# Layer 0: a term of TensorE's sum split between VectorE's partial sum and GpSimd's adds

## The chip, the cores and the metric

The kernel runs on one core of a Trainium2 chip. The metric is the device time of one execution in microseconds (us). The core has five engines that run their own instruction queues in order: TensorE (PE in the profile, with its weight loads as PEld), VectorE (DVE), ScalarE (ACT), GpSimd (POOL) and SyncE (SP), which here only issues transfers. They meet at semaphores.

## The reference, cut to what matters

Four layers are applied to x of shape (2, 64, 256, 256), each adding its result to x. The change is in layer 0. With _gn a group norm, _unfold3x3 nine copies of its input shifted by -2, 0 or 2 rows and columns (zero outside the image), and em an embedding of 64 channels made from an image and from positions:

```python
un_em = _unfold3x3(em)
feature_score = jnp.einsum('bckhw,bchw->bkhw', un_em, em)
un_fea = _unfold3x3(inp)
comp_score = jax.nn.sigmoid(jnp.einsum('bckhw,c->bkhw', un_fea, w_comp))
phi = comp_score * feature_score
weighted_fea = jnp.einsum('bckhw,bkhw->bchw', un_fea, phi)
...
x = x + _L0_conv_ref(_gn(x), L0_conv_img, L0_conv_w_pos, L0_conv_w_img, L0_conv_w_comp)
```

So for each of nine shifts the channels of em at a pixel are multiplied with those at the shifted pixel and summed to one score; the output is the sum over the shifts of score x g, where g is the input times its own sigmoid gate, taken at the shifted pixel.

## The kernel before, in words

The 128 partitions hold 2 images x 64 channels. Layer 0 goes over the image in 128 steps of two rows (nstep), so a tile of one step is 128 x 512 values, all float32. A score of a pixel and its neighbour is the same seen from either side, so of the nine shifts only five are computed: no shift, and A (0, 2), B (2, -2), C (2, 0), D (2, 2) in rows and columns (the dictionary shift). Each score of A to D is used twice. "term" is the score times g at the shifted pixel, for the pixel itself (mult, L366). "moved" is the score times the pixel's own g (move, L371), kept in padded tiles mvA to mvD, to be read later with the opposite shift (moved_to, L377) for the neighbour. A's neighbour is in the same two rows; those of B, C and D are in the next step's rows, so moved_to takes their tile of the step before.

One pass of the loop at L388 (index t) issues work of several stages:

- embed(t): TensorE's pl (L319) and pe (L321), ScalarE's sg and e (L325, L328), and at the end of the pass's GpSimd work the gate g = fea x sg (gated, L334). Every fourth step ScalarE first copies two halo rows of g and e (L317).
- products(t-2): ScalarE's square sq (L353), and on GpSimd the products of e with its four shifted views, pr (L356).
- step n = t-3: TensorE turns sq and the four pr into scores pf (score, L361: a matmul that sums over the channels of an image; it uses four PSUM buffers). VectorE multiplies: part = own g x score (L422), then for A, B, C, D the term and the moved tile. For A, VectorE also adds the term into part, in PSUM (L430), and then mvA and part into A's term tile (L431). So the shift of zero and both halves of A end in the one tile term A.
- step last = t-4: GpSimd adds the moved tile of the step before to the terms C, D and B, each in place (add, L381, in the order of L400). TensorE adds the four tiles A, C, D, B up in PSUM by matmuls with the identity (out, L405, tile acc). They are issued between the scores of step n. VectorE adds acc to x (yt, L438) and takes statistics (L439); yt goes out by a transfer (L440).

The order on every engine is the order in which these calls are written (L386 asks for a manual schedule). On GpSimd a pass is: C, D, B adds, four products, gate. On VectorE: part, A term, A moved, L430, L431, B term, B moved, C term, C moved, D term, D moved, yt, statistics: 13 operations. On TensorE: pl, pe, sq score, A score, acc A, B score, acc C, C score, acc D, D score, acc B: 11 matmuls. In float32 each shows as two matmul records and two weight loads.

part is one PSUM buffer, acc one, pf four. The term tiles come from a pool of 10, pr from 8, mvB, mvC and mvD from 3 each.

Of the kernel before, what the change touches and what calls it, by code (L numbers as in the profile page):

```python
# [18 lines left out]
C = 64  # L19
# [101 lines left out]
class Kernel:  # L121
# [115 lines left out]
    def layer0(self, x, y, coeffs):  # L237
# [3 lines left out]
        nc, tc, a = self.nc, self.tc, self.a  # L241
# [8 lines left out]
        with ExitStack() as ctx:  # L250
# [46 lines left out]
            xt, fea, sq, pr, term = {}, {}, {}, {}, {}  # L297
            inner = slice(2, 2 + W)

            def load(k):  # L300
                if 0 <= k < nblk:
                    xt[k] = pool.tile([P, R, W], F32, name="xt", bufs=3)
                    nc.sync.dma_start(xt[k], xv[:, R * k : R * k + R])
                    nc.sync.dma_start(rts[k % 2][32:38], rv[:, R * k : R * k + R])

            def features(n):
                k, s = divmod(n, per)
                fea[n] = pool.tile([P, 2, W], F32, name="fea")
                self.affine(fea[n], xt[k][:, 2 * s : 2 * s + 2], coeffs)

            def embed(n):
                k, s = divmod(n, per)
                g, e = gs[k % 2], es[k % 2]
                rows = slice(4 + 2 * s, 6 + 2 * s)
                if s == 0 and k:
                    for t in (gs, es):
                        nc.scalar.copy(t[k % 2][:, 2:4], t[1 - k % 2][:, R + 2 : R + 4])  # L317
                pl = p_l.tile([P, 2, W], F32, name="pl")
                nc.tensor.matmul(pl, wcomp, fea[n], start=True, stop=True)  # L319
                pe = p_e.tile([P, 2, W], F32, name="pe")  # L320
                nc.tensor.matmul(  # L321
                    pe, w_e, rts[k % 2][:, 2 * s : 2 * s + 2], start=True, stop=True
                )
                sg = pool.tile([P, 2, W], F32, name="sg")
                nc.scalar.activation(sg, pl, AF.Sigmoid)  # L325
                for i in range(2):
                    r = 2 * n + i
                    nc.scalar.activation(  # L328
                        e[:, 4 + 2 * s + i, inner],
                        pe[:, i],  # L330
                        AF.Identity,
                        bias=by_row[:, r : r + 1],
                    )
                return lambda: nc.gpsimd.tensor_tensor(  # L334
                    g[:, rows, inner], fea.pop(n), sg, ALU.mult
                )

            def at(n):

                k, s = divmod(n, per)  # L340
                if s == per - 1 and k + 1 < nblk:
                    return gs[(k + 1) % 2], es[(k + 1) % 2], 2
                return gs[k % 2], es[k % 2], 4 + 2 * s

            def near(t, j, name):
                dy, dx = shift[name]
                return t[:, j + dy : j + dy + 2, 2 + dx : 2 + dx + W]

            def products(n):
                _, e, j = at(n)  # L350
                own = e[:, j : j + 2, inner]
                sq[n] = pool.tile([P, 2, W], F32, name="sq")
                nc.scalar.activation(sq[n], own, AF.Square)  # L353
                for name in "ABCD":
                    t = pool.tile([P, 2, W], F32, name="pr", bufs=8)
                    nc.gpsimd.tensor_tensor(t, own, near(e, j, name), ALU.mult)  # L356
                    pr[n, name] = t

            def score(t):
                pf = p_f.tile([P, 2, W], F32, name="pf")  # L360
                nc.tensor.matmul(pf, self.block, t, start=True, stop=True)  # L361
                return pf

            def mult(n, name, in_, pf):
                t = pool.tile([P, 2, W], F32, name="term", bufs=10)
                nc.vector.tensor_tensor(t, in_, pf, ALU.mult)  # L366
                term[n, name] = t

            def move(n, name, own, pf):
                t = moved[name][n % len(moved[name])]  # L370
                nc.vector.tensor_tensor(t[:, :, inner], own, pf, ALU.mult)  # L371

            def moved_to(n, name):

                dy, dx = shift[name]
                n -= dy // 2
                return moved[name][n % len(moved[name])][:, :, 2 - dx : 2 - dx + W]  # L377

            def add(eng, n, name, other):
                t = term[n, name]  # L380
                eng.tensor_add(t, t, other)  # L381
# [4 lines left out]
            with tc.manual_schedule(engines={E.PE, E.DVE, E.Activation, E.Pool, E.SP}):  # L386
                features(0)
                for t in range(nstep + 5):  # L388
                    if t and t % per == 0:
                        load(t // per + 1)  # L390
                    gated = embed(t) if t < nstep else None
                    if t + 1 < nstep:
                        features(t + 1)

                    n, last = t - 3, t - 4
                    acc = None
                    if 0 <= last < nstep:
                        acc = p_o.tile([P, 2, W], F32, name="acc")
                        if last:
                            for name in "CDB":  # L400
                                add(nc.gpsimd, last, name, moved_to(last, name))

                    def out(name):
                        if acc is not None:
                            nc.tensor.matmul(  # L405
                                acc,
                                self.ident,
                                term.pop((last, name)),
                                start=name == "A",
                                stop=name == "B",  # L410
                            )

                    if 0 <= t - 2 < nstep:
                        products(t - 2)
                    if gated:
                        gated()
                    if 0 <= n < nstep:
                        g, _, j = at(n)
                        own = g[:, j : j + 2, inner]
                        pf = score(sq.pop(n))  # L420
                        part = p_s.tile([P, 2, W], F32, name="part")
                        nc.vector.tensor_tensor(part, own, pf, ALU.mult)  # L422
                        for i, name in enumerate("ABCD"):
                            pf = score(pr.pop((n, name)))
                            out("ACDB"[i])
                            mult(n, name, near(g, j, name), pf)
                            if name == "A" or n + 1 < nstep:
                                move(n, name, own, pf)
                            if name == "A":
                                nc.vector.tensor_add(part, term[n, name], part)  # L430
                                nc.vector.tensor_add(term[n, name], moved_to(n, name), part)  # L431
                    else:
                        for name in "ACDB":
                            out(name)
                    if acc is not None:
                        k, s = divmod(last, per)
                        yt = pool.tile([P, 2, W], F32, name="yt")
                        nc.vector.tensor_add(yt, xt[k][:, 2 * s : 2 * s + 2], acc)  # L438
                        nc.vector.bn_stats(stats[:, last, :], yt.rearrange("p r w -> p (r w)"))  # L439
                        nc.sync.dma_start(yv[:, 2 * last : 2 * last + 2], yt)  # L440
# [874 lines left out]
```

## Time and profile before

Three runs took 19660.62, 19662.92 and 19663.58 us: median 19662.92. The profiled execution took 19667.66 us, of which the span from its first to its last instruction is 19665.9.

| what | from the profile before |
|---|---|
| busy over the span | TensorE 74%, VectorE 94%, ScalarE 60%, GpSimd 82% |
| layer 0's steps | about 200 to 1458 us |
| adds of moved tiles (L381), GpSimd, 230 to 1440 us | mvC 1.09 us, mvD 1.27, mvB 1.27 each |
| products (L356), GpSimd | 1.13 us each on average |
| gate (L334), GpSimd | 1.27 us |
| VectorE's operations of a step | 0.68 to 0.70 us each |
| acc matmuls (L405), whole layer | 1024 records |
| granted TensorE clock, 300 to 1400 us | 1.00 |
| granted TensorE clock, whole span | 0.751 |

The page gives durations of single instructions as the profiler recorded them. Consecutive instructions of one engine overlap a little, so the pace of an engine is read from the distance between starts in the timeline, not from durations. In a line of the timeline the columns are start and length in us, engine, source line, operation, output <- inputs, form and count; a bracket at the end is the idle time before it and what ended it. Most of the span, some 14,000 us after layer 0, is layer 1, whose scan keeps VectorE busy; the shares over the whole span say little about layer 0.

### The profile page before, as it was taken

To read this page: it belongs to the slowest core of one execution; us is meant where nothing else is said; L and a number is where in the kernel's file an instruction comes from. 1 tells how busy PE (TensorE), PEld (TensorE's weight loads), DVE (VectorE), ACT (ScalarE), POOL (GpSimd) and SP (SyncE) were. 2 spreads that over 40 slices of the span, in tenths; PEclk is the share of its full clock that TensorE was granted. 3 is DMA by queue.
4 is the path that set the end of the run, shared out by engine and by line. 5 is a ranking of instruction groups with operands and counts; after the bars stand their busy time and mean duration, and the time that the engine had idled before them with its cause. 6 is when DMAs were issued, how large, how long until landed. Compare 5 with 4: busy or idle time off the path is not lost. (4 is left out here: it accounts for less than half of the span.)

```text
span 19665.9 us, 162715 instructions
## 1 busy us (share of the span) xinstructions
PE 14640.5 (74%) x48720; PEld 4861.7 (25%) x48720; DVE 18472.7 (94%) x16222; ACT 11804.0 (60%) x16810; POOL 16050.1 (82%) x8070
## 2 busy tenths in 40 slices
PE   7996767776777677767777677676777688888886
PEld 3431111111111111111111111111111154444444
DVE  6888999999999999999999999999999989999997
ACT  2226666666666666666666666666666555555554
POOL 6987888888888888888888888888888855555554
PEclk9996666666666666666666666666666698989898
DMA  3116666666666666666666666666666500000004
GB/s 124 54 50 157 151 151 151 153 149 156 149 154 152 151 151 151 155 147 157 151 153 150 151 152 151 156 148 154 154 150 151 126 28 29 30 30 29 29 27 145
DMA packets 662182, 2438.84 MB, mean 124 GB/s; under 512 B 131888, under 2 KB 201264, under 8 KB 450160
## 3 DMA queue, kind: packets, MB, share of 16 engines
q1 hardware_dynamic: 661296, 2428.43, 51.4%
q8 instruction: 385, 6.31, 0.1%
q14 instruction: 501, 4.10, 0.1%
HBM read 1990.14 MB, written 437.78 MB: 123 GB/s over the span
## 5 line engine op out<-in xcount | busy, mean ns | idle before, releaser
L792 DVE TENSOR_TENSOR_SCAN h<-da,st,h 128x512 f32<-128x512 f32 x8192 | 9838.6, 1263 | 308.2 <-ACT da L789 223.3
L796 POOL TENSOR_TENSOR h<-h,cb 128x2048 f32<-128x2048 f32 x2048 | 9253.1, 4518 | 164.9 <-POOL st L795 0.4
L789 ACT ACTIVATE da<-dl,p_a 128x512 f32<-128x512 f32 x8192 | 5565.3, 688 | 3985.5 <-DVE h L792 3891.2
L561 PE MATMUL py<-h,t_c_quad 128*32 128x512 f32 x16384 | 3253.7, 817 | 1649.1 <-POOL h L796 1648.6
L561 PE MATMUL pb<-bc,t_c_sel 64*128 64x512 f32 x3072 | 2697.0, 972 | 2385.5 <-DVE h L773 2379.9
L773 DVE TENSOR_TENSOR h<-dv,pb 128x2048 f32<-128x2048 f32 x1536 | 3472.3, 2261 | 40.9 <-DMA dv<-d_dv 40.9
L1021 POOL TENSOR_TENSOR gl<-gl,prod 128x512 f32<-128x512 f32 x1544 | 1959.0, 1270 | 1498.7 <-ACT prod L1017 1423.3
L755 POOL TENSOR_TENSOR h<-dv,cb 128x2048 f32<-128x2048 f32 x512 | 2318.7, 4529 | 17.1 <-DMA dl<-d_dl 17.1
L980 DVE SCALAR_TENSOR_TENSOR acc<-z,tap_b,acc 128x1024 f32<-128x1024 f32 (+1 forms) x1560 | 1988.4, 1275 | 38.8
L561 PEld LDWEIGHTS pb<-bc,t_c_sel 64*128 64x128 f32 x3072 | 661.6, 267 | 4411.3 <-DVE h L773 4345.9
L795 POOL COPY st<-h 128x4 f32<-128x4 f32 x2048 | 384.1, 188 | 1365.1 <-DVE h L792 1352.7
L561 PEld LDWEIGHTS py<-h,t_c_quad 128*32 128x32 f32 x16384 | 424.0, 122 | 3815.3 <-POOL h L796 3217.3
L561 PE MATMUL mm<-xin,p_conv 64*128 64x512 f32 x4096 | 1322.9, 775 | 15.2 <-DMA x1t<-y 15.2
L1064 PE MATMUL pcv<-z,diag 128*128 128x512 f32 x2322 | 1174.7, 623 | 19.8 <-ACT gl L1072 16.4
L949 ACT COPY z<-pz 128x512 f32<-128x512 f32 x768 | 456.4, 598 | 1034.1 <-PE pz L941 928.7
L1017 ACT ACTIVATE prod<-z,tap_a 128x512 f32<-128x512 f32 x1544 | 1045.1, 714 | 37.0 <-POOL gl L1021 36.8
L941 PE MATMUL pz<-t_c_inv,gf 128*128 128x128 f32 (+1 forms) x8192 | 1039.4, 309 | 1.9 <-DVE gf L922 1.9
L941 PEld LDWEIGHTS pz<-t_c_inv,gf 128*128 128x128 f32 (+1 forms) x8192 | 849.4, 181 | 520.0 <-issue 311.7
L561 PE MATMUL mm<-u,p_dt 128*128 128x512 f32 x1024 | 931.2, 1064 | 0.0
L561 PE MATMUL py<-u,p_d 128*128 128x512 f32 x1024 | 820.8, 894 | 0.0
L915 PE MATMUL f<-t_w_inT,xf 64*128 64x384 f32 x2048 | 596.7, 616 | 155.9 <-DVE gf L922 154.8
L561 PEld LDWEIGHTS mm<-xin,p_conv 64*128 64x128 f32 x4096 | 460.5, 244 | 982.6 <-issue 982.5
(167 smaller groups left out, 17448.8 us busy)
## 6 DMA issues: line engine op xcount, KB each, us to landing
cb<-d_bc SPq DMA_DIRECT2D x2048, 320.0 KB
dl<-d_dl SPq DMA_DIRECT2D x2048, 256.0 KB
dv<-d_dv SPq DMA_DIRECT2D x2048, 256.0 KB
d_dl<-delta SPq DMA_DIRECT2D x256, 512.0 KB
d_dv<-du SPq DMA_DIRECT2D x256, 512.0 KB
xin<-in_x SPq DMA_DIRECT2D x16, 2048.0 KB
xt<-in_x SPq DMA_DIRECT2D x32, 1024.0 KB
y<-yt SPq DMA_DIRECT2D x128, 256.0 KB
```

Source lines behind the costliest of these rows:

```text
L561: nc.tensor.matmul(out, lhsT, rhs, start=start, stop=stop)
L755: nc.gpsimd.tensor_tensor(h, t["dv", b], t["cb", b][:, 0].unsqueeze(1).to_broadcast([P, 4, T]), ALU.mult,)
L773: nc.vector.tensor_tensor(h, t["dv", b], pb.unsqueeze(1).to_broadcast([P, 4, T]), ALU.mult)
L789: nc.scalar.activation(da, t["dl", b][:, k], AF.Exp, scale=ws[m]["a"][:, k, j : j + 1])
L792: nc.vector.tensor_tensor_scan(h[:, k], da, h[:, k], state[m, b][:, j, k : k + 1], ALU.mult, ALU.add)
L796: nc.gpsimd.tensor_tensor(h, h, t["cb", b][:, 1 + j].unsqueeze(1).to_broadcast([P, 4, T]), ALU.mult)
L915: nc.tensor.matmul(p, x_f[t][half, g], w_in[half], start=True, stop=True)
L941: nc.tensor.matmul(pz[i * n : (i + 1) * n, k, :, 16 * g : 16 * g + 16], gf[t, 2 * e + g, b][:, c0 : c0 + n], inv, start=True, stop=True,)
L980: eng.scalar_tensor_tensor(out, near(s, name, m0, r, k), w, box["t"], ALU.mult, ALU.add)
L1017: nc.scalar.activation(prod, near(s, name, 4 * h + m, n, k), AF.Copy, scale=w)
L1021: nc.gpsimd.tensor_add(acc, acc, prod)
L1064: nc.tensor.matmul(box["t"], diag[:, k], near(s, f"a{i}", 4 * h + m, n, k), start=k == 0, stop=k == 8,)
```

## The change

B's term no longer has a tile of its own in TensorE's sum. In step n VectorE adds B's term to part in PSUM, as it does with A's. The add that makes the final A tile from mvA and part comes after that, behind B's term and B's moved tile. The moved tile of B, which GpSimd added to B's term, is now added to D's term, after mvD; GpSimd's adds stay three. TensorE sums A, C and D: A is issued behind the score of B instead of that of A, C behind that of C, D behind that of D, and D closes the sum.

```diff
-                            for name in "CDB":
-                                add(nc.gpsimd, last, name, moved_to(last, name))
+                            for name, moved_by in ("C", "C"), ("D", "D"), ("D", "B"):
+                                add(nc.gpsimd, last, name, moved_to(last, moved_by))
...
-                                stop=name == "B",
+                                stop=name == "D",
...
                         for i, name in enumerate("ABCD"):
                             pf = score(pr.pop((n, name)))
-                            out("ACDB"[i])
+                            if i:
+                                out("ACD"[i - 1])
                             mult(n, name, near(g, j, name), pf)
                             if name == "A" or n + 1 < nstep:
                                 move(n, name, own, pf)
-                            if name == "A":
+                            if name in "AB":
                                 nc.vector.tensor_add(part, term[n, name], part)
-                                nc.vector.tensor_add(term[n, name], moved_to(n, name), part)
+                            if name == "B":
+                                nc.vector.tensor_add(term[n, "A"], moved_to(n, "A"), part)
+                                term.pop((n, "B"))
                     else:
-                        for name in "ACDB":
+                        for name in "ACD":
                             out(name)
```

The tiles, pools and transfers are the same.

## The prediction

> **What bounds the kernel now.** The page says DVE 94% busy over the span, but that average belongs to layer 1. The change touches layer 0 alone, so I asked first for busy time by stretch, one stretch inside layer 0 and one inside layer 1. Columns: stretch, length, busy time of PE, PEld, DVE, ACT and POOL (with instruction counts), granted TensorE clock, DMA share, GB/s.
>
> ```profile
> 600.00:800.00 200.00, 200.00 (x449) 81.44 (x447) 168.02 (x266) 60.00 (x112) 185.57 (x163) 1.00 0.15 54
> 2000.00:3000.00 1000.00, 696.61 (x2052) 166.91 (x2052) 963.57 (x749) 655.27 (x893) 891.34 (x371) 0.69 0.66 152
> ```
>
> In layer 0 TensorE is busy 200 of 200 us at clock 1.00, GpSimd 93%, VectorE 84%. A busy TensorE isn't by itself a bound, so next the waits between 230 and 1440 us (total, times, longest):
>
> ```profile
> DVE part L422 <- PE pf L361: 148.1, 122, 1.2
> POOL term L381 <- DVE term L366: 84.2, 245, 0.4
> DVE term L366 <- PE pf L361: 19.9, 122, 0.2
> ```
>
> Once a step VectorE waits 1.2 us for TensorE's first score, and GpSimd waits twice for VectorE (0.28 and 0.41 us). TensorE's own waits (0.76 us ahead of the weights of pe and of sq) lie inside the 0.95 and 1.06 below. So the chain is TensorE, then VectorE, then GpSimd. TensorE's own timeline prices one step:
>
> ```profile
> 710.48 1.02 PE L319 MATMUL pl<-fea,wcomp 128*128 128x512 f32 x2
> 711.43 1.12 PE L321 MATMUL pe<-rt,w_e 38*128 38x512 f32 x2
> 712.49 1.13 PE L361 MATMUL pf<-sq,t_c_block 128*128 128x512 f32 x2
> 713.45 1.02 PE L361 MATMUL pf<-pr,t_c_block 128*128 128x512 f32 x2
> 714.31 1.02 PE L405 MATMUL acc<-term,t_c_ident 128*128 128x512 f32 x2
> ...
> 720.32 1.02 PE L319 MATMUL pl<-fea,wcomp 128*128 128x512 f32 x2
> ```
>
> Starts matter here, not durations: 0.86 from one matmul to the next, but 0.95, 1.06 and 0.96 after pl, pe and the sq score. 8 x 0.86 + 2.97 = 9.84 us, the step's period.
>
> **TensorE: one matmul fewer.** The acc matmul of B goes (two records of 0.43): 9.84 - 0.86 = 8.98 us. If nothing else were near, 122 steps x 0.86 = 105 us would go. The other two engines decide how much of it is kept.
>
> **VectorE: one add more.** Of its 13 operations it now does 14: B's term is added to part (L430's form), and the add that makes A's term moves behind B. Its pace without waits shows at the end of the layer, where TensorE has less to do (timeline of DVE, the same instruction one step apart, no wait recorded):
>
> ```profile
> 1430.18 0.68 DVE L422 TENSOR_TENSOR part<-g,pf 128x512 f32<-128x512 f32 x1
> 1430.77 0.68 DVE L366 TENSOR_TENSOR term<-g,pf 128x512 f32<-128x512 f32 x1
> ...
> 1438.20 0.68 DVE L422 TENSOR_TENSOR part<-g,pf 128x512 f32<-128x512 f32 x1
> ```
>
> 8.02 us for 13 operations: 0.60 each, 0.72 where an operation reads the result just made (L430 to L431, 1431.97 to 1432.69). The new add reads part and a term made two operations earlier, so it costs 0.60; the 0.72 stays once, in front of the last add. 8.62 us, 8.74 if the new add pays 0.72 as well. A rule speaks against this: the Trainium skill, "VectorE: DVE Perf Modes", section "The DRAIN you can't avoid", says that the next operation doesn't start until the pipe is empty, and gives 691 ns for such an fp32 add. By the rule a step is 14 x 0.69 = 9.66 us and nearly the whole gain is gone; by the row it is 8.62. The row decides: it is this loop, and 13 x 0.69 = 8.97 would not fit in its 8.02.
>
> **GpSimd: the same three adds, but two of them on one tile.** It did C+mvC, D+mvD, B+mvB; now C+mvC, D+mvD, D+mvB. Its timeline over one step:
>
> ```profile
> 707.61 1.28 POOL L334 TENSOR_TENSOR g<-fea,sg 128x512 f32<-128x512 f32 x1
> 709.16 1.09 POOL L381 TENSOR_TENSOR term<-term,mvC 128x512 f32<-128x512 f32 x1 [0.27 <-DVE term L366]
> 710.65 1.26 POOL L381 TENSOR_TENSOR term<-term,mvD 128x512 f32<-128x512 f32 x1 [0.41 <-DVE term L366]
> 711.88 1.26 POOL L381 TENSOR_TENSOR term<-term,mvB 128x512 f32<-128x512 f32 x1
> 713.11 4.37 POOL L356 TENSOR_TENSOR pr<-e 128x512 f32<-128x512 f32 x4
> 717.44 1.27 POOL L334 TENSOR_TENSOR g<-fea,sg 128x512 f32<-128x512 f32 x1
> ```
>
> An instruction that waits for nothing starts some 0.04 before the end of the one ahead. So from start to start: C 1.05 (its 1.09 less 0.04), D 1.23, B 1.23, four products 4.33, gate 1.23: 9.07 us without its waits. The third add now reads what the second just wrote. Layer 2 has such chains on GpSimd, of the same size:
>
> ```profile
> 16829.97 10.79 POOL L1021 TENSOR_TENSOR gl<-gl,prod 128x512 f32<-128x512 f32 x8 [3.92 <-ACT prod L1017]
> ```
>
> (10.79 - 1.28) / 7 = 1.36 from start to start, 0.13 more than 1.23. That gives 9.20 us. Bounds: 9.07 if the dependence is free (it can't be a gain, the operations being the same), 9.25 if it costs what D now pays behind VectorE (its start comes 0.14 after the end of the multiply at 719.66 + 0.69: 1.27 + 0.14 = 1.41). I take 9.20, the nearest row.
>
> So the three floors are 8.98, 8.62 and 9.20: **GpSimd becomes the bound**, and keeps 0.63 of the 0.86.
>
> **Do the queues let it run there?** TensorE issues in order, so a late GpSimd tile stops it. With pl of a TensorE step at 0: D's score at 7.25, VectorE's C multiply (0.6 later than now, behind the new add) at 8.3, D's at 9.5; GpSimd's next round of adds starts at 9.1 and ends at 12.9; the last acc matmul of the next TensorE step, which now waits for D's second add, stands at 8.98 + 8.11 = 17.1. That is 4.2 us of slack. Being 0.22 slower per step, GpSimd uses it up in about 20 steps; from then on TensorE waits some 0.2 us a step in front of its last acc matmul, with the next step's pl, pe and scores behind it, and VectorE's part behind those. VectorE has 0.5 us to spare. ScalarE's halo copy (every fourth step) waits for the gate, which comes later relative to TensorE; the next fea is then ready about 1.2 us before its pl needs it. Score buffers: the tightest, B's, is freed at 9.6 and needed at 12.8. The y and x transfers stay as they are, at 15% DMA share. The accumulation of A moves from the first to the second place in TensorE's order: nothing, A's last add was made a step before.
>
> **The sum.** GpSimd's C add runs from 217.49 to 1426.99 us, 123 steps at 9.83. 123 x (9.83 - 9.20) = 77.5. Added: at the end TensorE is 4.6 us ahead of GpSimd's C add instead of 1.3 behind, +5.9. Taken off: VectorE's first C multiply 0.6 later, and two closing steps at VectorE's pace, 2 x 0.60. Together 77.5 + 5.9 - 0.6 - 1.2 = 82 us. Layers 1 to 3 get the same instructions, only earlier: 0. The profiled execution took 19667.7 us (span 19665.9), so 19586; the median shown is 4.7 lower, so **19581 us**, 0.42% faster. About 0.2%, 39 us, can be told from no change.
>
> **Rivals.** (1) *TensorE stays the bound*: GpSimd would have to do its step in under 8.98, below even its 9.07 without any dependence. 105 less the 1.8 of start and end: 19560. Against it: GpSimd's products take 4.36 us for four at 192.92, when VectorE has not yet begun, and 4.37 in the loop, so no hidden stretch there will shrink. (2) *VectorE becomes the bound*, at the skill's 9.66: 122 x 0.17 = 21 us less, 19642, no change that can be told. For it: 14 operations, and TensorE's score for A holds the second of them back now (0.16). Against it: the 8.02. (3) *The clock falls*, the case on the slow side. TensorE is at clock 1.00 while it never pauses; afterwards it pauses once a step. Its period is 8.57 / clock + 0.40, over 9.83 once the clock is below 0.91. Layer 1's row above, 70% busy, shows 0.69: 12.8 us, 122 x 3.0 = 366 us more, 20029. The skill, "TensorE: Matmul & The Clock Gate", section "What's actually happening", lets the clock fall only after an idle window of some 3.4 us; by that rule a pause of 0.2 us costs nothing. The row of layer 1 can't decide, its pauses being longer; the stretch from 95 to 165 us, with pauses and 89% busy, has clock 1.00. So I follow the rule, without certainty. That the change doesn't do what it says can be left out: the number of matmuls follows from the loop.
>
> **Chances and range.** GpSimd bound 0.77, TensorE bound 0.07, VectorE bound (no change) 0.08, clock or some stall of that size 0.08. Faster 0.84, same 0.08, slower 0.08. The likeliest case spans 9.07 to 9.25 us: 19565 to 19587. The range takes in the TensorE case below, and above it a GpSimd step up to 9.40, in case waits inside its queue remain: 123 x 0.43 + 4 = 57 us, 19606. So 19555 to 19607.
>
> **What would show it.** Right: 256 fewer acc records on TensorE; clock still 1.00; the step near 9.2 from C add to C add; GpSimd 99% busy with its waits for VectorE nearly gone; 1.36 between the two adds on D; in TensorE's waits a new one for term L381, 0.2 a step. Wrong: VectorE without waits (rival 2), TensorE without waits (rival 1), a clock below 1.00 (rival 3), or GpSimd still waiting for VectorE at a period over 9.3, which would mean that the lead I give TensorE can't build up.

## The result and the profile after

Six runs of the changed kernel took 19578.54 to 19587.15 us, median 19582.24. Six runs of the kernel before had a median of 19663.25. The ratio is 0.9959, 95% interval 0.9946 to 0.9972: 81 us or 0.41% faster, where 19581 us had been forecast. The profiled execution took 19581.46 us (span 19579.7), 86.2 less than that of before.

First by stage. The group norm after each layer begins with one aggregate of statistics on VectorE. These are its rows in the kernel before, for layers 0, 1 and 2 (timeline of DVE):

```profile
1459.23 3.60 DVE L159 BATCH_NORM_AGGREGATE mv<-stats 128x2 f32<-128x768 f32 x1
...
15721.43 3.62 DVE L159 BATCH_NORM_AGGREGATE mv<-stats 128x2 f32<-128x768 f32 x1
...
19340.07 3.65 DVE L159 BATCH_NORM_AGGREGATE mv<-stats 128x2 f32<-128x774 f32 x1
```

and in the changed kernel:

```profile
1377.17 3.62 DVE L159 BATCH_NORM_AGGREGATE mv<-stats 128x2 f32<-128x768 f32 x1
...
15637.53 3.62 DVE L159 BATCH_NORM_AGGREGATE mv<-stats 128x2 f32<-128x768 f32 x1
...
19255.44 3.65 DVE L159 BATCH_NORM_AGGREGATE mv<-stats 128x2 f32<-128x774 f32 x1
```

Layer 0 ends 82.1 us earlier. The lead then grows to 83.9 and 84.6: layers 1 and 2, which got the same work, came out 1.8 and 0.7 us shorter in this one execution. The runs of the changed kernel spread over 9 us, so these few microseconds are nothing to explain.

Inside layer 0, the busy time of the same stretch as before (columns as there):

```profile
600.00:800.00 200.00, 200.00 (x436) 77.32 (x436) 190.39 (x306) 63.68 (x118) 198.35 (x176) 1.00 0.17 60
```

GpSimd went from 185.57 to 198.35 of 200 us, VectorE from 168 to 190. TensorE still reads 200 of 200, at clock 1.00, though it is no longer what sets the pace: the records of neighbouring matmuls overlap by 0.16 us (1.02 long, 0.86 apart), and a wait of 0.1 us disappears in that overlap. GpSimd's timeline shows the pace:

```profile
705.46 1.27 POOL L334 TENSOR_TENSOR g<-fea,sg 128x512 f32<-128x512 f32 x1
706.69 1.08 POOL L381 TENSOR_TENSOR term<-term,mvC 128x512 f32<-128x512 f32 x1
707.74 1.26 POOL L381 TENSOR_TENSOR term<-term,mvD 128x512 f32<-128x512 f32 x1
709.08 1.27 POOL L381 TENSOR_TENSOR term<-term,mvB 128x512 f32<-128x512 f32 x1
710.31 4.38 POOL L356 TENSOR_TENSOR pr<-e 128x512 f32<-128x512 f32 x4
714.65 1.26 POOL L334 TENSOR_TENSOR g<-fea,sg 128x512 f32<-128x512 f32 x1
715.88 1.08 POOL L381 TENSOR_TENSOR term<-term,mvC 128x512 f32<-128x512 f32 x1
```

No bracket is left: GpSimd waits for no other engine. (Some 0.08 us stand in front of the second add on D, too short for a bracket; 21.8 steps of them are the 1.65 us that 198.35 lacks of 200.) From C add to C add it is 9.19 us, and the second add on D starts 1.34 after the first, where two adds on different tiles started 1.23 apart before. The waits from 230 to 1340 us (total, times, longest) agree:

```profile
PEld acc L405 <- POOL term L381: 83.0, 111, 0.8
...
DVE part L422 <- PE pf L361: 21.6, 104, 0.2
DVE term L366 <- PE pf L361: 19.6, 121, 0.2
```

GpSimd's waits for VectorE (84.2 us before) are gone from the list. VectorE's wait at part shrank from 1.2 to 0.2 us a step. New is TensorE's wait for a GpSimd add ahead of an acc matmul, 111 times. The 0.8 is counted on the weight loads and holds their normal 0.24 and more. What it costs is read from TensorE's starts. Here are step ends around the first such wait, and one in the middle of the layer:

```profile
370.62 1.02 PE L405 MATMUL acc<-term,t_c_ident 128*128 128x512 f32 x2
371.48 1.02 PE L319 MATMUL pl<-fea,wcomp 128*128 128x512 f32 x2
...
378.73 1.02 PE L361 MATMUL pf<-pr,t_c_block 128*128 128x512 f32 x2
379.59 1.12 PE L405 MATMUL acc<-term,t_c_ident 128*128 128x512 f32 x2
380.55 1.02 PE L319 MATMUL pl<-fea,wcomp 128*128 128x512 f32 x2
...
709.43 1.02 PE L361 MATMUL pf<-pr,t_c_block 128*128 128x512 f32 x2
710.40 1.12 PE L405 MATMUL acc<-term,t_c_ident 128*128 128x512 f32 x2
711.37 1.02 PE L319 MATMUL pl<-fea,wcomp 128*128 128x512 f32 x2
```

The step that begins with the pl at 362.50 is 8.98 us long (to 371.48), as all were since 218.90. The one after it is 9.07, and from the step behind it on some 0.97 stands in place of 0.86 on both sides of the last acc matmul (709.43, 710.40, 711.37), 0.21 a step together. So for some 18 steps TensorE ran at its own 8.98 and drew ahead, and then it was held.

### The profile page after: what moved, and what is told of

The parts are those of the page before. It is cut to its first block, busy times and chain, and to the rows that moved or that the text cites. A ratio compares the mean times of both kernels' runs of the same rounds, so it can differ in the third digit from the quotient of the medians.

```text
span 19579.7 us, 162084 instructions
## 1 busy us (share of the span) xinstructions
PE 14539.7 (74%) x48464; PEld 4804.5 (25%) x48464; DVE 18532.4 (95%) x16350; ACT 11806.1 (60%) x16810; POOL 16045.7 (82%) x8070
```

## The experiments

All are edits of the changed kernel, except e6, which edits the kernel before. The kernel before ran beside each group at medians of 19660 to 19667, so times of different groups compare only to within a few microseconds; against the kernel before that ran beside it, the change alone gains 81.0 us.

**e1, the two adds on D apart.**

```diff
-for name, moved_by in ("C", "C"), ("D", "D"), ("D", "B"):
+for name, moved_by in ("D", "D"), ("C", "C"), ("D", "B"):
```

> The changed kernel with GpSimd's adds in the order D+mvD, C+mvC, D+mvB, so that the two adds on D no longer follow each other. Theory (GpSimd is the bound, and 0.13 us of its step is the wait of the second add on D for the first): the step from C add to C add falls from 9.19 to 9.06 us, 123 steps x 0.13 = 16 us less, about 19566. Rival (the step is set by TensorE and VectorE waiting for each other, GpSimd only follows): step 9.19 as it was, 19582. Second rival (the second add on D is slow for another reason than its neighbour): also 9.19.

Measured: 19570.64 us, ratio 0.9951 (0.9937 to 0.9966). GpSimd's timeline of e1:

```profile
699.21 1.26 POOL L381 TENSOR_TENSOR term<-term,mvD 128x512 f32<-128x512 f32 x1
700.44 1.08 POOL L381 TENSOR_TENSOR term<-term,mvC 128x512 f32<-128x512 f32 x1
701.48 1.26 POOL L381 TENSOR_TENSOR term<-term,mvB 128x512 f32<-128x512 f32 x1
...
708.28 1.26 POOL L381 TENSOR_TENSOR term<-term,mvD 128x512 f32<-128x512 f32 x1
```

The step is 9.07. The same three adds in another order are 0.12 us a step shorter, so what stood between the adds on D was the one waiting for the other. The time followed: 94.4 us under the kernel before that ran beside it, 13.4 more than the change alone, where 123 x 0.12 makes 14.8 and the expectation said 16. So GpSimd was the bound.

**e2, GpSimd's third add left out.**

```diff
-for name, moved_by in ("C", "C"), ("D", "D"), ("D", "B"):
+for name, moved_by in ("C", "C"), ("D", "D"):
```

> The changed kernel without GpSimd's third add (B's moved twin is left out of the output). Theory: GpSimd's floor falls to 9.19 - 1.35 = 7.84 us, TensorE becomes the bound with 8.98 us, its 10 matmuls: 122 x 0.86 = 105 us less than before, less 2 at the ends: about 19560; VectorE's part waits for TensorE 0.1 us or less. If VectorE sets the step: 9.19, 19582. If one GpSimd operation was worth its whole 1.35: 19416, which TensorE can't follow.

Measured: 19556.67 us, ratio 0.9944 (0.9929 to 0.9959). The pl matmul stands at 700.93 and 709.91, a step of 8.98, and GpSimd waits again (its timeline):

```profile
701.06 1.09 POOL L381 TENSOR_TENSOR term<-term,mvC 128x512 f32<-128x512 f32 x1 [0.94 <-DVE term L366]
```

Of the 1.35 us taken off GpSimd only 0.21 shows in the step: the next floor is TensorE's.

**e3, one part of the change alone.** B's term joins part on VectorE; B's moved tile goes straight into TensorE's sum, which keeps four tiles.

```diff
-for name, moved_by in ("C", "C"), ("D", "D"), ("D", "B"):
+for name, moved_by in ("C", "C"), ("D", "D"):
...
-                                term.pop((last, name)),
+                                moved_to(last, "B") if name == "B" else term.pop((last, name)),
...
-                            if i:
-                                out("ACD"[i - 1])
+                            out("ACDB"[i])
```

> One part of the change alone: B's term joins part on VectorE, with the later final add of A, but B's moved tile goes as a fourth tile into TensorE's sum and GpSimd has two adds. Theory: TensorE's 11 matmuls bound the step at 9.84 us as before, with VectorE at 14 operations hidden behind them: 19663 (19658 to 19668). Rival (the gain comes from VectorE's new order or from GpSimd, not from the matmul removed): step under 9.3, 19590 or less. Rival (14 operations cost VectorE 9.66 us and more): step at or over 9.84, with VectorE not waiting for TensorE at all; under the theory its part waits about 0.6 us a step.

Measured: 19666.43 us, ratio 1.0001 (0.9993 to 1.001). Two of its waits from 230 to 1340 us (columns as above):

```profile
POOL term L381 <- DVE term L366: 202.9, 113, 1.8
...
DVE part L422 <- PE pf L361: 96.0, 113, 0.9
```

GpSimd has an add less and VectorE one more, and nothing moves: pl stands at 708.39 and 718.22, a step of 9.83. GpSimd's saved time turned into a wait of 1.8 us. VectorE's part waits 0.85 at 14 operations; a VectorE at 9.66 could not. (The expected 0.6 left out a second wait of the kernel before, 0.22 us in front of D's term: it starts 0.82 behind the operation ahead there, at 709.00 and 709.82, and 0.60 in e3. 1.21 - 0.60 + 0.22 = 0.83.) So the gain of the change is the matmul's, not that of VectorE's new order or of GpSimd.

**e4, e8, e9, where the moved tiles begin.** The tiles of B and D are made wider and written a few columns further right, and read there; d is 2 in e4, 4 in e8, 1 in e9 (the tiles of e8 and e9 are 8 columns wider instead of 4).

```diff
-                    keep.tile([P, 2, W + 4], F32, name=f"mv{n}{i}", tag=f"mv{n}{i}")
+                    keep.tile([P, 2, W + 4 + 4 * (n in "BD")], F32, name=f"mv{n}{i}", tag=f"mv{n}{i}")
...
-                nc.vector.tensor_tensor(t[:, :, inner], own, pf, ALU.mult)
+                lo = 2 + d * (name in "BD")
+                nc.vector.tensor_tensor(t[:, :, lo : lo + W], own, pf, ALU.mult)
...
-                return moved[name][n % len(moved[name])][:, :, 2 - dx : 2 - dx + W]
+                lo = 2 + d * (name in "BD") - dx
+                return moved[name][n % len(moved[name])][:, :, lo : lo + W]
```

> The changed kernel with the moved tiles of B and D laid out two columns further right in wider tiles, nothing else. In the trace GpSimd's two-input operations take 1.05 us from start to start where the two inputs begin at different places modulo 16 bytes and 1.23 where they begin at the same (term with mvC 1.05; term with mvD or mvB 1.23; the product with C's view 1.24, with the other three 1.00 to 1.05; the gate 1.23). Theory (the place of the inputs decides): both adds on D take 1.09 us instead of 1.27, GpSimd's floor falls by 0.36 to 8.83, TensorE bounds at 8.98: about 19560. Rival (the differences have another cause, such as the buffers or what runs beside them): adds stay at 1.27, step 9.19, 19582.

> The changed kernel with the moved tiles of B and D four columns (16 bytes) further right instead of two (8 bytes). Theory (what counts is whether both inputs of a GpSimd operation begin at the same place modulo 16 bytes): as in the changed kernel, both adds on D take 1.27 us, step 9.19, about 19582. Rival (any other place or the wider tiles make the adds faster, as two columns did): 1.09 us, step 8.98, 19559.

> The changed kernel with the moved tiles of B and D one column (4 bytes) further right. Theory (any difference modulo 16 bytes is enough): adds of about 1.09 us, step 8.98, 19559. Rival (only half a line, 8 bytes, is): adds of 1.27, step 9.19, 19582; a value between would say that the distance itself counts.

Measured: e4 19559.01 us (ratio 0.9945, 0.9929 to 0.9962), e8 19578.67 (0.9958, 0.9938 to 0.9977), e9 19552.80 (0.9946, 0.9923 to 0.9968). GpSimd's adds in the timelines of e4:

```profile
711.89 1.09 POOL L383 TENSOR_TENSOR term<-term,mvC 128x512 f32<-128x512 f32 x1
713.08 1.09 POOL L383 TENSOR_TENSOR term<-term,mvD 128x512 f32<-128x512 f32 x1
714.25 1.09 POOL L383 TENSOR_TENSOR term<-term,mvB 128x512 f32<-128x512 f32 x1
```

one of e9:

```profile
703.41 1.09 POOL L383 TENSOR_TENSOR term<-term,mvD 128x512 f32<-128x512 f32 x1
```

and of e8:

```profile
707.28 1.09 POOL L383 TENSOR_TENSOR term<-term,mvC 128x512 f32<-128x512 f32 x1
708.32 1.27 POOL L383 TENSOR_TENSOR term<-term,mvD 128x512 f32<-128x512 f32 x1
709.67 1.27 POOL L383 TENSOR_TENSOR term<-term,mvB 128x512 f32<-128x512 f32 x1
```

A shift by 8 bytes takes 0.18 us off each add, by 4 bytes as well (e9), by 16 bytes nothing: e8 gains 81.6 us on the kernel before beside it, as the change alone does. So neither the wider tile nor a new place does it, but the inputs beginning at different places modulo 16 bytes. In e4 and e9 the step is 8.98 (e9's pl at 702.08 and 711.06), TensorE's floor again, by a way that leaves no work out. GpSimd has time to spare in it: in e4 it starts D's add 1.19 behind C's instead of 1.05, because VectorE's term of D ends only at 713.01. The chain of two adds on D stays (1.17 from start to start instead of 1.05): the price of the dependence is 0.12 here too.

**e5, a fifteenth operation on VectorE.**

```diff
+                            if name == "C":
+                                extra = pool.tile([P, 2, W], F32, name="extra")
+                                nc.vector.tensor_tensor(extra, own, pf, ALU.mult)
```

> The changed kernel with a fifteenth operation on VectorE in each step: C's moved product once more, into a tile that nobody reads. Theory (an operation costs VectorE 0.60 us from start to start, and it has some 0.5 us to spare behind GpSimd): its floor rises from 8.62 to 9.22 us, just level with GpSimd's 9.19: step 9.19 to 9.25, time 19582 to 19592. Rival (an operation keeps VectorE for its full 0.69 us): 15 x 0.69 = 10.35, step 1.16 more, 19725. Rival (VectorE and TensorE already set the step together): the whole 0.60 x 125 = 75 us more, 19657.

Measured: 19595.11 us, ratio 0.9963 (0.995 to 0.9976). In its timeline of DVE:

```profile
701.62 0.68 DVE L422 TENSOR_TENSOR part<-g,pf 128x512 f32<-128x512 f32 x1
...
710.85 0.68 DVE L422 TENSOR_TENSOR part<-g,pf 128x512 f32<-128x512 f32 x1
```

No bracket: VectorE doesn't wait, and fifteen operations take it 9.22 us. That is the expected floor, and 130 us away from what 0.69 an operation would give. The time is 3 us above the expected range, for two reasons. The expectation took the middle of the layer for the whole: in the changed kernel VectorE's 127 distances from part to part have a mean of 9.135 (205.41 to 1365.57), because the first ones go at TensorE's 8.98 or below and the last at 8.62; here all but the first are 9.22. That makes 10.6 us. Another 3.3 came up behind the last part. There VectorE stands in front of a copy for the next layer, until a transfer lands (timeline of DVE):

```profile
1388.07 0.26 DVE L493 COPY p_dt_in<-t_p_xproj_dt 4x128 f32<-4x128 f32 x1 [5.69 <-DMA t_p_xproj_dt<-in_p_xproj_dt]
```

The last yt comes behind this copy, at 1388.25, though its acc is done at 1384.92; in the changed kernel it comes ahead of the copy. So these 3.3 us belong to the transfer and not to the fifteenth operation.

**e6, the kernel before with pe on 128 rows.** Weights and data of pe are padded with zero rows.

```diff
-            w_e = keep.tile([38, P], F32, name="w_e")
+            w_e = keep.tile([P, P], F32, name="w_e")
...
-            rts = [keep.tile([38, R, W], F32, name=f"rt{i}", tag=f"rt{i}") for i in range(2)]
+            rts = [keep.tile([P, R, W], F32, name=f"rt{i}", tag=f"rt{i}") for i in range(2)]
             for t in rts:
+                nc.vector.memset(t, 0.0)
```

> The kernel before with the pe matmul on 128 rows instead of 38, the added rows of weights and data being zero. In the timeline the matmuls around pe start 0.95, 1.06 and 0.96 us after one another instead of 0.86. Theory (the pause belongs to the change of the row count, and TensorE is the bound of the kernel before): 0.10 + 0.20 + 0.10 = 0.40 us of the step goes, 9.84 to 9.44, 123 x 0.40 = 49 us less: about 19616. Rival (the pause is a wait for ScalarE or for a buffer): step 9.84, 19665. Rival (GpSimd or VectorE bounds the kernel before): also 19665.

Measured: 19614.96 us, ratio 0.9974 (0.9963 to 0.9984). TensorE's timeline of e6:

```profile
703.72 1.02 PE L320 MATMUL pl<-fea,wcomp 128*128 128x512 f32 x2
704.58 1.02 PE L322 MATMUL pe<-rt,w_e 128*128 128x512 f32 x2
705.44 1.02 PE L362 MATMUL pf<-sq,t_c_block 128*128 128x512 f32 x2
706.30 1.02 PE L362 MATMUL pf<-pr,t_c_block 128*128 128x512 f32 x2
```

0.86 everywhere: the 0.40 us around pe is gone, the next pl stands at 713.16, a step of 9.44, and 52 us went with it. That the kernel before was bound by TensorE is shown from a second side, by an edit that touches no other engine's share of the step.

**e7, all together:** e1's order, e4's tiles, e6's rows, and the second input of the gate moved right by two columns.

```diff
-                sg = pool.tile([P, 2, W], F32, name="sg")
+                sg = pool.tile([P, 2, W + 2], F32, name="sg")[:, :, 2:]
```

> The changed kernel with all that lowers a floor: adds on D apart, moved tiles of B and D two columns right, the gate's second input two columns right, pe on 128 rows. Theory (each engine's floor is the sum of its distances from start to start): GpSimd 4.33 + 3 x 1.05 + 1.05 = 8.53, TensorE 10 x 0.86 = 8.57, VectorE 8.62: VectorE becomes the bound, step 8.62 to 8.75, 123 x 0.3 = 37 us less than with the shifted tiles alone: about 19520. Rival (with three floors so near one another the waits between the engines keep the step where it is): 8.98, 19559.

Measured: 19514.07 us, ratio 0.9922 (0.9905 to 0.9938), faster than both kernels: 153 us under the kernel before that ran beside it (19666.85), where the change alone gains 81. Its timeline of DVE:

```profile
700.64 0.68 DVE L425 TENSOR_TENSOR part<-g,pf 128x512 f32<-128x512 f32 x1
...
709.27 0.68 DVE L425 TENSOR_TENSOR part<-g,pf 128x512 f32<-128x512 f32 x1
```

The step is 8.62, VectorE's floor for 14 operations to the hundredth, without a wait. But GpSimd, worked out at 8.53, shows no wait either: it is busy 200 of the 200 us from 600 to 800. Its gate is dearer than the expectation had it, already ahead of the loop, where nothing holds it (timeline of POOL, two gates and the products behind them):

```profile
190.53 2.31 POOL L335 TENSOR_TENSOR g<-fea,sg 128x512 f32<-128x512 f32 x2
192.79 4.36 POOL L357 TENSOR_TENSOR pr<-e 128x512 f32<-128x512 f32 x4
```

(192.79 - 190.53) / 2 = 1.13 from start to start, 1.14 in the loop, not 1.05. 4.33 + 3 x 1.05 + 1.14 = 8.62: GpSimd's floor is as high as VectorE's, and the run does not tell which of the two sets the step. It shows that the step comes down to the highest floor, with TensorE's worked-out 8.57 close below. The 1.14 fits e4, e8 and e9: the tile of sg is now 258 columns or 1032 bytes wide, so only the first of its two rows begins at another place modulo 16 bytes than fea's, and half at 1.05 and half at 1.23 makes 1.14. That is worked out; no run tests it.

## Why the prediction was right

- **The bound before.** TensorE, by its starts: shown by e3 (an add less on GpSimd and one more on VectorE, no change) and e6 (0.40 us off TensorE, the step 0.40 shorter).
- **TensorE's 8.98.** Measured in the changed kernel before TensorE is held, and as the bound in e2 and e4.
- **VectorE's 8.62.** Between 1348.33 and 1356.95, at the end of the layer, 14 operations take 8.62, and in e7 all through it. The rule that a next operation starts only when the pipe is empty would have made 9.66 of it, a step over the 9.19 measured. The row was right to decide, and the rule was read by half: the section of the Trainium skill that the prediction names, "The DRAIN you can't avoid", goes on to say that a next operation that is not held starts earlier, here 0.60 us after the one ahead instead of 0.69.
- **GpSimd's 9.20.** Measured 9.19; 1.34 for the dependent add against 1.36 from layer 2's chain. It is the bound: e1, e2 and e4 each shorten GpSimd alone, and each shortens the step, e1 to GpSimd's own 9.07, e2 and e4 down to TensorE's floor and no further; e8, which shortens nothing, leaves the step at 9.19.
- **The slack of 4.2 us, used up in about 20 steps.** Used up after some 18. At the end of the layer, TensorE's first step without pl and pe begins at 1345.46 and GpSimd's C add at 1349.96: 4.5 us ahead, where 4.6 was expected.
- **The sum.** Measured, 123 steps x (9.833 - 9.191) = 79.0; TensorE's lead 5.8; the first C add 1.95 later (0.9 of it a set-up that began that much later, 1.07 the term put at 0.6); the rest, about -0.8, falls to the closing steps. Together 82.1, from aggregate row to aggregate row; the forecast was 82.
- **The clock.** 1.00 from 300 to 1340 us, with a pause in every step. The case on the slow side did not come up, and pauses of 0.2 us did not bring the clock down here. What a lower clock would have cost in the loop no run shows.

The mechanism came out as forecast. That the sum fits to half a microsecond is in part luck, for its terms were off and cancel: the pace gave 1.5 us more than its term (0.642 a step instead of 0.63), the closing steps cost 0.4 less, and the first C add took 1.35 more, 0.9 of it from the later set-up, for which the forecast had no term.

## What to carry to other kernels

Work out a floor for each engine as the sum of its distances from start to start, not of its durations, and take those distances from stretches where the engine waits for nothing: the layer's last steps gave VectorE's, TensorE's own row gave TensorE's. What the removal of work on the bound is worth is the distance to the next floor (0.63 of 0.86 us here), and the next floors say where to look afterwards: in e7, a reorder and shifted tiles on GpSimd and 90 zero rows on TensorE were worth some 70 us more. A short lead that one engine builds over another before it is held is a term of its own, here 6 us of 82.

## What was not expected of the hardware

- A GpSimd operation with two inputs of 128x512 float32 takes 1.27 us when both begin at the same place modulo 16 bytes and 1.09 when they don't, for 4 or 8 bytes of difference alike (12 were not tried). The Trainium skill, "SBUF — State Buffer", section "Specifications (TRN2)", speaks of 16-byte lines in SBUF with a price for each change of line; that the two inputs changing lines together is the cause fits, but no run here shows it.
- A matmul on 38 rows between matmuls on 128 costs TensorE 0.40 us beyond its 0.86, at its own start and at the two that follow; with zero rows added up to 128 it costs nothing (e6).
